# Windowed linear attention: masking part of the score lists by a product on VectorE in place of bias matmuls

## The chip, the cores and the metric

The kernel runs on one core of one Trainium2 chip. The metric is the time of one execution on the device in microseconds (us); lower is better. Engines are called PE (TensorE, its weight loads as PEld), DVE (VectorE), ACT (ScalarE), POOL (GpSimd) and SP (SyncE, here only a queue of DMAs).

## The reference

Two layers work on an image of 256 channels and 64 x 64 pixels in f32. Layer 0 is a windowed linear attention with a projection; layer 1 is a causal softmax attention over the 4096 pixels as tokens, with a feed-forward part, and then a mixture of experts. Only layer 0 is touched here. Cut to its core:

```python
q, k = sigmoid(Wq x), sigmoid(Wk x)             # 8 heads of 32 channels
v = Wv x;  v = v / max(norm(v), 1e-12)
Ik, Ikv = integral(k), integral(k v^T)          # sums over rows and columns
for w in (1, 2, 4):                             # window sides 64, 32, 16
    ws = 64 // w
    attn = q . box(Ikv, ws) / (q . box(Ik, ws) + 1e-6)
out = x + Wout concat(attn) + bout
```

For every query pixel this is the sum of (q.k) v over all key pixels inside a square window, divided by the sum of q.k.

## The kernel before, in words

The kernel doesn't form the box sums of k v^T at every pixel. It multiplies queries with the keys near the border of their window and then with the values, as an attention does, and takes what is entirely inside the windows from sums over blocks of 8 x 8 pixels. Only the border work is changed here.

**Head groups and stages.** `window_heads` runs twice, for heads 0 to 3 and 4 to 7. Each time it projects q, k and v, and then goes through two stages of border work. The *column stage* (windows of half 16 and 32, `beside`) treats key blocks at the left and right border. Its results go through DRAM (`store`, SP). The *row stage* (`above`, windows of half 8, 16, 32) treats the upper and lower border in eight strips of 8 image rows, Y = 0 to 7, and finishes each strip.

**Parts and lists.** A `Part` is one tile of 128 keys against a rectangle of 124 to 256 queries. `packed` puts two to three parts into a *list* of at most 512 queries, so that one head's scores of a list fill one PSUM bank. There are 44 lists in the column stage and 91 in the row stage of each head group, 135 in all, so 270 in the kernel. A part with `half` set has only half a tile of keys.

**`push(parts)`** handles one list. It takes four PSUM banks, one for each head. For each part and head it issues first a bf16 matmul (line 428) that writes a bias into the bank: 0 where the key lies in the query's window, at least -64 below it where not (`window_tables`). Then it issues the f32 score matmul (line 441), which adds q.k. Each f32 matmul stands in the trace as two records. Since q.k is positive and below 64, a ReLU of the sum leaves q.k inside the window and 0 outside. `evacuate` (lines 387 to 392) does that ReLU from PSUM into the buffer `pm`, one instruction for each head: five of eight on ACT, three of eight on DVE. `pm` shares a pool of three buffers (tag "work") with the raw image.

**`add()`** multiplies the oldest waiting `pm` with the values (line 474) into an accumulator bank. In `push`, `if len(waiting) > 1: add()` makes the products of a list follow the scores of the next one on PE. When an accumulator is complete, `finish` (row stage, DVE lines 506 and 509, POOL line 510) or `store` (column stage, ACT line 486) empties it.

**PSUM.** `Banks` hands out eight banks in turn. An accumulator holds one, so that about seven rotate. `push` takes four each time, and a bank can be written again when what was in it has been read.

**Order.** In these stages the order of PE, POOL, DVE and ACT is that of the program (`manual_schedule`); SP's order is set by the framework. In the row stage `plan(at, ...)` puts further work behind given lists: `outer` (DMAs of the column results), `inner` (block sums for a strip, DVE lines 574 to 582), `ahead` (box sums, POOL), `quarters` (DMAs of values), the steps of `norms` (PE, ACT, four DVE reciprocals of line 555), `convolve` (the projection of the strip before, PE line 589 and DVE line 594) and, in the second head group only, the layer norm of the strip before (`causal.measure`, `root`, `norm`, `turn`, `sum_up`). `spread_out` copies norms from PSUM (line 564).

**Memory that the change reuses.** The weights `l0Wq`, `l0Wk`, `l0Wv` are not read after the projections of a head group, nor is `going`, the start pattern of the running sums of line 614. A DMA for the next head group's image (`raw`) goes into a buffer of the pool "work".

## Time and profile before

| | us |
|---|---|
| time of three runs: median (lowest to highest) | 1775.1 (1774.4 to 1779.42) |
| the profiled execution: its time | 1775.84 |
| its span, first to last instruction | 1774.0 |
| column stage, first and second head group | about 82 to 178, 500 to 592 |
| row stage, first and second head group | about 178 to 437, 592 to 865 |
| layer 1 | from about 902 to the end |

The mean granted TensorE clock is 0.984 of full speed. Times in a profile are counted from the first instruction. A row of a group gives the line, engine and operation, out<-in, the count, the busy time (us) and the mean of one (ns), and behind the bar the idle time just before. Instructions of one engine can overlap by some ten ns, so that a group's busy time can be less than count times mean.

### The profile page before, as it was taken

The page shows a single profiled execution, that of the slowest core. Times are in us where ns is not written, and L with a number is a line of the kernel's source. Part 1 is how long each engine was busy: PE and PEld are TensorE (multiplying, and loading weights), DVE is VectorE, ACT ScalarE, POOL GpSimd, SP SyncE. Part 2 cuts the span into 40 slices and gives each one's busy share as a digit, 9 for nine tenths or more (in the row PEclk, how much of TensorE's full clock was granted, in tenths as well). Part 3 has the DMA queues.
Part 4 walks back from the last instruction along what each step waited for, and adds up shares of the span by engine and source line. Part 5 has one row for each costly group of instructions (what it writes and reads, how often), then busy time and mean ns, then how long its engine had stood idle before and what let it go on. Part 6 is the DMA issues. An engine that isn't in the chain of part 4 may idle for free.

```text
span 1774.0 us, 48097 instructions
## 1 busy us (share of the span) xinstructions
PE 1697.7 (96%) x20940; PEld 1252.7 (71%) x20940; DVE 989.3 (56%) x2002; ACT 789.5 (45%) x1478; POOL 518.7 (29%) x783
## 2 busy tenths in 40 slices
PE   4999999999999999999999999999999998699998
PEld 3666666666666666666777888788777777477877
DVE  5645666665744677777633446455655565634434
ACT  2566444444456644545223334444444445332232
POOL 2386434441274353333110312212112111122211
PEclk9999999999999999999999999999999998799999
DMA  7521211001331210002000000000000000100000
GB/s 241 138 74 50 57 28 38 20 21 48 125 91 44 73 28 24 24 22 73 3 0 1 1 0 1 1 1 0 1 0 1 1 1 1 48 12 24 13 24 24
DMA packets 82915, 61.13 MB, mean 34 GB/s; under 512 B 39120, under 2 KB 72808, under 8 KB 82704
## 3 DMA queue, kind: packets, MB, share of 16 engines
q1 hardware_dynamic: 77776, 47.61, 9.3%
q10 hardware_dynamic: 3664, 6.61, 1.1%
q0 software_dynamic: 1264, 3.84, 0.7%
q8 instruction: 164, 2.69, 0.6%
q14 instruction: 47, 0.39, 0.1%
HBM read 40.60 MB, written 17.44 MB: 33 GB/s over the span
## 4 chain that ended last, share of the span: by engine, by line
PE 87%; DVE 6%; ACT 3%; DMA 2%; issue 1%; POOL 0%; ACTq 0%; SPq 0%; DVEq 0%; POOLq 0%
PE ps L474 14%; PE ps L441 12%; PE pa L1162 11%; PE po L1235 10%; PE ph L1572 6%; PE py L1592 6%; PE ps L589 5%; PE ps L428 5%; PE ps L601 3%; PE ps L494 2%; PE pm L1296 2%; PE pm L1091 2%; PE ps L624 2%; PE pm L1305 1%; PE ps L560 1%
## 5 line engine op out<-in xcount | busy, mean ns | idle before, releaser
L390 ACT ACTIVATE pm<-ps 128x448 f32<-128x448 f32 (+22 forms) x674 | 323.7, 545 | 278.7 <-PE ps L441 163.0
L392 DVE TENSOR_SCALAR pm<-ps 128x448 f32<-128x448 f32 (+13 forms) x406 | 240.8, 621 | 202.9 <-PE ps L441 132.7
L441 PE MATMUL ps<-q,kh 32*128 32x188 f32 (+15 forms) x4224 | 205.7, 332 | 0.3 <-issue 0.3
L1162 PE MATMUL pa<-qT,k 128*128 128x256 f32 (+1 forms) x800 | 184.7, 375 | 0.0
L1178 DVE TENSOR_TENSOR max<-max,pa 128x512 f32<-128x512 f32 x105 | 71.8, 684 | 189.4 <-ACT s L1174 189.3
L1162 PEld LDWEIGHTS pa<-qT,k 128*128 128x128 f32 x800 | 150.2, 190 | 23.5 <-issue 2.2
L1214 ACT ACTIVATE s<-s 128x512 f32<-128x512 f32 x136 | 85.5, 630 | 179.2 <-DVE s L1213 175.5
L441 PEld LDWEIGHTS ps<-q,kh 32*128 32x128 f32 (+1 forms) x4224 | 145.4, 169 | 6.7 <-issue 4.2
L474 PE MATMUL ps<-pm,vh 128*32 128x188 f32 (+9 forms) x2688 | 148.4, 336 | 0.0
L510 POOL TENSOR_TENSOR y<-y,rn 128x512 f32<-128x512 f32 x32 | 41.1, 1283 | 329.1 <-DVE y L509 324.4
L1174 ACT COPY s<-pa 128x512 f32<-128x512 f32 x120 | 69.8, 582 | 114.9 <-PE pa L1162 114.8
L428 PE MATMUL ps<-table,table 32*128 32x256 bf16 (+19 forms) x2752 | 120.3, 252 | 0.0
L428 PEld LDWEIGHTS <-table 32*128 32x128 bf16 (+1 forms) x2752 | 48.0, 94 | 98.9 <-issue 96.0
L1592 PE MATMUL py<-w,hT 128*128 128x256 f32 x512 | 111.8, 379 | 0.0
L1592 PEld LDWEIGHTS py<-w,hT 128*128 128x128 f32 x512 | 97.3, 190 | 15.7 <-issue 1.9
L474 PEld LDWEIGHTS ps<-pm,vh 128*32 128x32 f32 x2688 | 71.1, 109 | 52.5 <-issue 34.7
L1235 PE MATMUL po<-kh,s 128*128 128x257 f32 x406 | 105.5, 388 | 2.4 <-ACT s L1214 2.4
L1213 DVE TENSOR_TENSOR s<-s,tops 128x512 f32<-128x512 f32 x136 | 95.2, 703 | 1.0 <-ACT tops L1206 1.0
L589 PE MATMUL ps<-l0wo,y 128*128 128x256 f32 x384 | 90.7, 387 | 0.0
L1235 PE MATMUL po<-v,s 128*128 128x257 f32 x342 | 87.6, 387 | 1.8 <-ACT s L1214 1.8
L1235 PEld LDWEIGHTS po<-kh,s 128*128 128x128 f32 x406 | 75.9, 194 | 15.9 <-ACT s L1214 3.8
L1597 DVE TENSOR_TENSOR y<-py,xn 128x256 f32<-128x256 f32 x32 | 13.6, 425 | 131.0 <-issue 78.1
(325 smaller groups left out, 3028.8 us busy)
## 6 DMA issues: line engine op xcount, KB each, us to landing
oscratch<-ov SPq DMA_DIRECT2D x32, 256.0 KB
ov<-oscratch SPq DMA_DIRECT2D x32, 256.0 KB
vq<-vscratch SPq DMA_DIRECT2D x80, 64.0 KB
t<-in_xT SPq DMA_DIRECT2D x16, 256.0 KB
vscratch<-v SPq DMA_DIRECT2D x32, 128.0 KB
vh<-vscratch SPq DMA_DIRECT2D x16, 256.0 KB
raw<-in_x ACTq DMA_DIRECT2D x7, 512.0 KB
raw<-in_x SPq DMA_DIRECT2D x7, 512.0 KB
```

The costliest lines, as they stand in the source:

```text
L390: nc.scalar.activation(dst, src, AF.Relu)
L392: nc.vector.tensor_scalar_max(dst, src, 0.0)
L428: nc.tensor.matmul(got[h][ps, spot].rearrange("p (y x) -> p y x", y=part.r1 - part.r0), lhsT=spread[hs, kind, ks], rhs=bias[hs], start=(i ...
L441: nc.tensor.matmul(got[h][ps, spot].rearrange("p (y x) -> p y x", y=part.r1 - part.r0), lhsT=keys[hs], rhs=q[hs, part.r0 : part.r1, part.c ...
L474: nc.tensor.matmul(out, lhsT=v, rhs=pm[:, h, spot].rearrange("p (y x) -> p y x", y=part.r1 - part.r0), start=fresh, stop=(left[key] == 0), ...
L589: nc.tensor.matmul(pt[:, i * D : (i + 1) * D], lhsT=ys[wi, Y][:, (2 * j + i) * P : (2 * j + i + 1) * P], rhs=wo[:, n, :], start=(n == 0), ...
L1162: nc.tensor.matmul(pp[:, k * 2 * P + at : (k + 1) * 2 * P], lhsT=key, rhs=qT[:, c, q0 + at : q0 + 2 * P], start=(c == 0), stop=(c == DC - 1))
L1213: nc.vector.tensor_tensor(s, s, u["top"].unsqueeze(1).to_broadcast([P, 2, 2 * P]), op=ALU.subtract)
L1214: nc.scalar.activation(u[b], u[b], AF.Exp, scale=1.0 / 16.0)
L1235: nc.tensor.matmul(acc, lhsT=u[b][:, (2 * k + j) * P : (2 * k + j + 1) * P], rhs=v[2 * b + k][:, 0 : D + 1], start=(b == h and k == 0), st ...
L1572: nc.tensor.matmul(ph, lhsT=w1v[:, e, c, f, :], rhs=x2[g][c], start=(c == 0), stop=(c == DC - 1))
L1592: nc.tensor.matmul(py, lhsT=hT[:, e, f, j * P : (j + 1) * P], rhs=w2v[:, e, f, :], start=(e + f == 0), stop=(e == 1 and f == FC - 1))
```

## The change

Of each head group's 135 lists, 60 are *masked*: 21 of the column stage (every second one from the third on) and 39 of the row stage (a list without half parts, never two in a row). For a masked list `push` issues no bias matmul; the first score matmul starts the bank. It is evacuated by DVE alone, with one `tensor_mul` for each part and head: scores in PSUM times a mask of bytes (1 inside, 0 outside) into `pm`. Each of the other 75 lists is evacuated by ACT alone, four ReLUs. The split of `evacuate` is gone.

The masks come from DRAM, five DMAs on SP's queue before the column stage's first list and one before the row stage, in each head group: into the memory of the weights (three), of `going` (two), and into a tile `near` of its own. The second head group fills `going` again (two memsets).

The products now follow two lists behind the scores (`len(waiting) > 2`), so all three buffers of "work" are in use. Between the stages the waiting products of the column stage are issued at once. In the row stage `outer` and `quarters` come one list later, and `convolve` with all that is chained to it too.

```diff
+MASKS = ("near", "beside 1", "beside 2", "beside 4", "above 1", "above 2")
+def inside_or_not():
+    spread, *tables = [o[0:32].astype(np.float32) for o in window_tables()]
+    kinds = [(0, tables[0]), (1, tables[3]), (1, tables[4]), (2, tables[5]), (0, tables[1]), (0, tables[2])]
+    masks = [np.tensordot(spread[:, kind], o, (0, 0)) == 0 for kind, o in kinds]
+    for n in (4, 5):
+        masks[n] = np.stack([masks[n][:, 0, 0:4, 16:-16], masks[n][:, 1, 4:8, 16:-16]], 1)
+    return masks
 def window_masks():
-    return window_tables()
+    return [*window_tables(), np.concatenate([m.reshape(P, -1) for m in inside_or_not()], 1).astype(np.uint8)]
...
+    shapes, masks = dict(zip(MASKS, inside_or_not())), {}
+    def load_mask(name, dst):
+        sizes = [int(np.prod(shapes[n].shape[1:])) for n in MASKS[: MASKS.index(name) + 1]]
+        dst = dst[:, 0 : sizes[-1]]
+        masks[name] = dst.rearrange("p (s y x) -> p s y x", s=shapes[name].shape[1], y=shapes[name].shape[2])
+        nc.sync.dma_start(out=dst, in_=a["mask7"][:, sum(sizes[:-1]) : sum(sizes)])
+        return sizes[-1]
+    def inside_of(part):
+        r, c = part.r0 + part.b0, part.c0 + part.d0
+        if part.vertical:
+            m = masks["beside 4" if part.half is not None else f"beside {part.wi}"]
+        elif part.wi == 0:
+            m = masks["near"]
+        else:
+            m, r, c = masks[f"above {part.wi}"], part.r0 % 4, c - 16
+        return m[:, part.side, r : r + part.r1 - part.r0, c : c + part.c1 - part.c0]
...
+    if hg:
+        nc.vector.memset(going, 1.0)
+        nc.vector.memset(going[:, :, 0:1], 0.0)
...
-    def push(parts):
+    def push(parts, masked=False):
...
-        for i, (part, spot) in enumerate(order):
+        for i, (part, spot) in enumerate([] if masked else order):
...
-                        start=False, stop=(i == len(parts) - 1), skip_group_check=True,
+                        start=(masked and i == 0), stop=(i == len(parts) - 1), skip_group_check=True,
...
         for h in range(4):
-            evacuate(pm[:, h, 0:at], got[h][:, 0:at])
+            if masked:
+                for part, spot in zip(parts, spots):
+                    rows = lambda s: s.rearrange("p (y x) -> p y x", y=part.r1 - part.r0)
+                    nc.vector.tensor_mul(rows(pm[:, h, spot]), rows(got[h][:, spot]), inside_of(part))
+            else:
+                nc.scalar.activation(pm[:, h, 0:at], got[h][:, 0:at], AF.Relu)
         waiting.append((parts, spots, pm))
-        if len(waiting) > 1:
+        if len(waiting) > 2:
             add()
...
+            for name, o in zip(("beside 1", "beside 2", "beside 4"), ws):
+                load_mask(name, o.rearrange("p c e -> p (c e)").bitcast(U8))
+            unused = going.rearrange("p y x -> p (y x)").bitcast(U8)
+            n = load_mask("above 1", unused)
+            load_mask("above 2", unused[:, n:])
             lists = packed(list(beside(wi, X)) for X in range(8) for wi in (1, 2))
...
-                push(parts)
+                push(parts, i % 2 == 1)
...
             push(lists[0])
+            while len(waiting) > 1:
+                add()
             by_rows(2)
             by_rows(3)
...
+        load_mask("near", h.tile([P, shapes["near"][0].size], U8, name="near"))
+        masked = [0]
+        for n in range(3, len(lists)):
+            if n > masked[-1] + 1 and all(part.half is None for part in lists[n]):
+                masked.append(n)
...
-            plan(at, lambda Y=Y: (outer(1, Y), outer(2, Y)))
+            plan(at + (1 if Y else 0), lambda Y=Y: (outer(1, Y), outer(2, Y)))
...
-                plan(at, lambda Y=Y: (ahead(Y + 1), quarters(Y + 1)))
+                plan(at, lambda Y=Y: ahead(Y + 1), lambda Y=Y: quarters(Y + 1))
...
-                end = plan(at + 3, *(lambda j=j, Y=Y: convolve(Y - 1, j) for j in range(2)))
+                end = plan(at + 4, *(lambda j=j, Y=Y: convolve(Y - 1, j) for j in range(2)))
...
-                push(parts)
+                push(parts, n in masked)
```

More of the change, by code (lines that the diff above doesn't have):

```diff
@@ L16 @@
 I32 = mybir.dt.int32
+U8 = mybir.dt.uint8
 AF = mybir.ActivationFunctionType
@@ L383, in window_heads @@
     ikv = big.tile([P, 9, 9, 32], F32, name="ikv")
-    counter = [0]
-    def evacuate(dst, src):
-        counter[0] += 1
-        if counter[0] % 8 in (1, 3, 5, 7, 0):
-            nc.scalar.activation(dst, src, AF.Relu)
-        else:
-            nc.vector.tensor_scalar_max(dst, src, 0.0)
     accs, left, state, ys, waiting = {}, {}, {}, {}, []
```

## The prediction

> **What bounds the kernel now.** I read the page first, then the busy time by stage, then the order in time of a few lists, and at last the groups that the change touches.

> ```profile
> PE 1697.7 (96%) x20940; PEld 1252.7 (71%) x20940; DVE 989.3 (56%) x2002; ACT 789.5 (45%) x1478; POOL 518.7 (29%) x783
> PE 87%; DVE 6%; ACT 3%; DMA 2%; issue 1%; POOL 0%; ACTq 0%; SPq 0%; DVEq 0%; POOLq 0%
> ```

> PE is busy 96% of the span, and the chain that ended last runs over it for 87%. That is a mean over stages. The four stages that the change touches (column and row stage of each head group) read so; behind the stretch stand its length and the busy time of PE, PEld, DVE, ACT and POOL:

> ```profile
> 82.00:178.00 96.00, 93.66 (x2094) 60.44 (x2096) 47.39 (x79) 63.44 (x133) 70.86 (x127) 0.98 0.19 61
> 178.00:437.00 259.00, 258.99 (x5847) 170.61 (x5846) 161.35 (x263) 120.89 (x247) 96.49 (x113) 1.00 0.13 31
> 500.00:592.00 92.00, 89.74 (x1982) 57.89 (x1986) 43.13 (x71) 59.15 (x123) 46.04 (x106) 0.96 0.19 60
> 592.00:865.00 273.00, 272.70 (x6028) 180.22 (x6023) 198.09 (x372) 132.76 (x274) 99.38 (x115) 1.00 0.15 37
> ```

> PE has no hole in either row stage. DVE is busy 62% and 73% there, 49% and 47% in the column stages. The order in time of a few lists on PE shows what a list consists of:

> ```profile
> 116.78 0.41 PE L428 MATMUL ps<-table,table 32*128 32x160 bf16 x12
> 117.03 1.04 PE L441 MATMUL ps<-q,k 32*128 32x168 f32 x24
> 118.00 0.96 PE L474 MATMUL ps<-pm,v 128*32 128x224 f32 x16
> 118.89 0.40 PE L428 MATMUL ps<-table,table 32*128 32x256 bf16 x8
> 119.12 0.98 PE L441 MATMUL ps<-q,k 32*128 32x224 f32 x16
> 120.03 1.05 PE L474 MATMUL ps<-pm,v 128*32 128x160 f32 x24
> 121.01 0.40 PE L428 MATMUL ps<-table,table 32*128 32x256 bf16 x8
> ```

> Bias, scores and products follow without a wait for the evacuation. What a bias costs is start to start: 119.12 - 118.89 = 0.23 us for two parts, 117.03 - 116.78 = 0.25 for three. Over all lists with nothing else between, these are 0.207 (8 matmuls) and 0.247 (12).

> **1. The removed bias matmuls.** Over both head groups 92 masked lists have two parts and 28 have three: 92 x 0.207 + 28 x 0.247 = 26.0 us of PE, all on the path. That is the upper end. The first weight load of a list is now that of a score, 185 ns (median of line 441) in place of 93 ns (line 428), and nothing may run under it: at worst 120 x 0.092 = 11.0 us come back, so the lower end is 15. I take half, **20.5 us gained**.

> **2. DVE's new work.** The nearest rows are DVE's present evacuation, and line 509, a tensor_tensor of PSUM with SBUF:

> ```profile
> 116.08 1.16 DVE L392 TENSOR_SCALAR pm<-ps 128x448 f32<-128x448 f32 x2 [1.43 <-PE ps L441]
> 300.28 0.68 DVE L509 TENSOR_TENSOR y<-ps,ov 128x512 f32<-128x512 f32 x1
> 300.87 0.94 DVE L555 RECIPROCAL r<-r 96x128 f32<-96x128 f32 x1
> ```

> One evacuation of 448 columns has a mean of 622 ns, yet two in a row take 1.16 us: the second starts 0.54 after the first. From the starts of such pairs the pitch is 441 ns at 352 columns, 541 at 448, 608 at 512: **73 ns + 1.045 ns a column**. The tensor_tensor behaves alike: 0.68 long, but the next starts 0.59 after it. Its 32 executions take 679 to 693 ns, so a busy POOL doesn't slow this form. A read of bytes isn't in the trace; I take f32's pace, since the same row holds for one tensor or two.

> A masked list of two parts of 224 then takes 4 x 2 x (0.073 + 0.234) = 2.46 us of DVE. The masked lists of a head group hold 46 + 88 parts and 9496 + 17504 columns: 184 x 0.073 + 37984 x 1.045 ns = 53.1 us in the column stage, 352 x 0.073 + 70016 x 1.045 ns = 98.9 in the row stage. The present evacuation leaves: 40.7 and 38.8 us of DVE in the column stages, 78.8 and 81.5 in the row stages. DVE becomes 59.8 of 96, 181.5 of 259, 57.4 of 92 and 215.5 of 273 us: 62%, 70%, 62%, 79%. So DVE doesn't become the bound on the mean.

> [...]

> **3. When banks come free.** Before, a list's four banks were emptied by two engines in some 1.2 us; now one engine takes 2.5 (DVE) or 4 x 0.44 = 1.8 (ACT, from its pitch of 441 ns at 448 columns). With seven banks rotating, the scores of list n+2 need three of list n's banks and one of n+1's. Two lists of 448 columns take PE 2 x 2.0 - 0.2 = 3.8 us by the rows above, scores last about 0.9, so the need comes 2.9 us after the end of list n's scores; DVE is done at about 2.5 + 0.1. That is 0.3 to 0.4 of slack for each masked list. The second list of lag covers the products: list n's come after the scores of n+2. So strict alternation costs nothing by itself. What is queued on DVE behind a masked list does: `inner` (3.1 us for both windows in the first strip), four reciprocals (0.94 each), `finish` (0.6 each), `convolve`'s add (0.6 each), and in the second head group the layer norm, (198.1 - 81.5) - (161.4 - 78.8) = 34 us, some 5 a strip.

> I walked through strip Y = 2 (lists 20 to 32, six masked). Lists 20-21: DVE 3.9, PE 4.9 us. 22-23, with `inner`: DVE 5.4 to 6.8, PE 3.9. 24-25: DVE 3.4, PE 9.0, as `convolve` (2.8 x 2) now lies there and hides most of the backlog; about 0.4 is lost. 26-27 and 28-29: DVE 4.5, PE 5.0. 30-32: DVE 5.8, PE 5.6. So 0.3 to 0.4 us is lost in a strip of the first group: 2 us in all. In the second, 26-27 and 28-29 become 5.9 on DVE against 5.0 and 5.1, which loses another 0.5 and 0.8 in the three strips with six masked lists: 5 us in all. The column stages have only `norms`' reciprocals near their end and the turns of accumulators: 1 us.

> **4. Queues.** Five mask DMAs stand on SP before the first list. A DMA issue of this queue takes some 0.6 us, and the nearest small one, 64 KB into `kh`, lands 2.88 us after its issue at 90.65. The first masked list's product is due at about 92, so DVE, and behind it PE, can wait up to 3 us in each head group if the masks lie behind `kh`, and nothing if the framework puts them ahead: 0 to 6 us, I take 2. `raw` for the second head group waits for a buffer of "work" one list longer; PE idles for it today (about 439.6 to 442.3): 0 to 2 us, I take 1. `outer`, `quarters` and `near` are covered: `finish` for `ov` comes eight lists, some 16 us, later; without that cover one landing of about 3 us would show. Filling `going` again is under 1 us of DVE before the scans, while PE waits for `raw` anyway. The changed place of `convolve` costs nothing of its own. ACT evacuates with 300 instructions a head group in place of 337, so it is no bound.

> **The sum.** -20.5 + 2 + 5 + 1 + 2 + 1 = -9.5 us. From the profiled 1775.84 that is 1766.3; the median of the runs lies 0.7 below the profiled one, so **1766 us**.

> **Rivals.**
> - *Everything is hidden.* The backlog vanishes in places where PE does other work, the masks are early, the weight load overlaps: 26 - 2 = 24 us gained, **1751**. For it: DVE at 70 to 79% and slack in every pair. Against it: the bursts of strip Y = 2.
> - *Bank release becomes the wait (slower).* DVE is in order, and one `inner` or two reciprocals in front of a masked list hold four banks. If each of the 14 strips with such bursts loses 2.3 us (one `inner` of 1.5 to 2.4 us and some rest) in place of 0.5, that is 32 us: 1775 - 20.5 + 32 + 3 = **1790**. It decides from 1.3 us a strip on. The same comes about if the products run at their full duration (143 ns + 1.06 a column, from the same rows) and not at the pitch: a masked list then takes 3.2 us, over the 2.9 that PE leaves. For it: DVE's 79% is a mean, and in three strips of the second group it is near 90% (strip Y = 2, 661 to 699 us: DVE 29.2 busy, 11.2 of it evacuation, 15.2 in its place, so 33.2 of 38 - 1.2).
> - *No net change.* The lower end of the saving, 15 us, meets 10 to 15 us of waits, late masks among them: **1774**.

> **How the numbers follow.** The forecast has 0.38, all hidden 0.15, bank release 0.32, no net change 0.15. A measurement tells about 0.3% (5.3 us) from no change. The forecast's own range is 1758 to 1773. Faster by more: 0.30 of the forecast and all of the second case, 0.45. Within 0.3%: the forecast's remainder and the last case, 0.23. Slower: 0.32. The range reaches to the case with all hidden below, and to the slower case with 2 us on top: 1751 to 1792.

> **What the profile would show.** Line 428 falls from 2752 to 1680 records. The product comes as a DVE group of 1072 instructions with 224 columns at about 0.31 us of pitch. If step 1 is right, the start of a masked list's score follows the products with no more than 0.1 us beyond today's 0.25. If step 3 is right, PE stays over 97% busy in the row stages, and the second is the worse one. If the slower rival is right, PE shows waits before line 441 that end with DVE's product, most of them behind lines 574 to 582 and 555. A masked list that waits for a DMA in the first 15 us of a column stage would show step 4. Wrong would be: a pitch over 0.36 us for 224 columns, or a second column stage that grows.

## The result, and the profile after

| | before | after |
|---|---|---|
| median of four runs each (us) | 1775.97 (1774.4 to 1779.42) | 1835.79 (1831.82 to 1837.91) |
| ratio, with its 95% interval | | 1.0331 (1.0307 to 1.0356) |
| profiled execution: time, span (us) | 1775.84, 1774.0 | 1831.82, 1830.0 |
| mean granted TensorE clock | 0.984 | 0.975 |

The change made the kernel slower by 3.3%, some 60 us. The forecast was 1766, and its range ended at 1792.

Line numbers from here on are those of the changed kernel: bias 456, score 469, masked product 479, ACT's ReLU 481, products with the values 507, `finish` 542 (DVE) and 543 (POOL), box sums 556 to 571, copy of the norms 597, `convolve` 622 and 627.

The head of the page of the changed kernel:

```profile
span 1830.0 us, 46546 instructions
PE 1717.3 (94%) x19868; PEld 1264.9 (69%) x19868; DVE 1050.5 (57%) x2670; ACT 744.8 (41%) x1404; POOL 518.1 (28%) x783
```

PE has 1072 records fewer and is nevertheless busy 19.6 us longer: the matmuls themselves became slower. The stages, in the columns that the prediction used (stretch, length, busy time of PE, PEld, DVE, ACT and POOL, granted clock, DMA share, GB/s):

```profile
82.00:175.00 93.00, 89.20 (x1838) 57.36 (x1838) 58.80 (x191) 52.57 (x109) 67.92 (x120) 1.00 0.20 66
175.00:464.00 289.00, 272.65 (x5534) 180.35 (x5530) 184.45 (x481) 108.44 (x231) 98.22 (x118) 0.96 0.11 28
529.00:623.00 94.00, 89.57 (x1839) 57.66 (x1832) 59.88 (x194) 53.00 (x111) 48.19 (x111) 1.00 0.20 63
623.00:917.00 294.00, 279.21 (x5559) 184.34 (x5559) 205.61 (x572) 116.69 (x248) 97.69 (x114) 0.97 0.14 34
```

The column stages changed by less than 2 us. The row stages grew from some 261 and 269 us to 289 and 293. PE was without a hole in them before (0.3 us in both); now it stands idle for 16 and 15 us, and the granted clock fell to 0.96 and 0.97 on the mean. DVE, the engine that received the new work, is busy 64% and 70% there: it is not the bound.

Three rows of the waits (who waited <- for whom; the engine's idle time before it in us in total, times, longest) name the place. The last two are the same waits, seen on PE's weight loads and on its matmuls:

```profile
ACT rn L597 <- POOL y L543: 67.9, 12, 8.2
PEld ps L469 <- ACT rn L597: 29.2, 10, 4.4
PE ps L469 <- ACT rn L597: 26.5, 10, 4.1
```

None of them existed before. There ACT's copy of the norms waited for PE's norms, and a few times for less than 0.8 us for something else; and POOL's multiply of `finish` stood ahead of the box sums (a row of the waits, and two rows in time of the same strip, from the kernel before):

```profile
ACT rn L564 <- PE ps L560: 21.9, 26, 1.2
```

```profile
234.90 1.29 POOL L510 TENSOR_TENSOR y<-y,rn 128x512 f32<-128x512 f32 x1 [6.71 <-DVE y L509]
236.14 1.29 POOL L525 TENSOR_TENSOR rows<-ik 128x520 f32<-128x520 f32 x1
```

Now ACT's copy waits for POOL's multiply, and the scores wait for ACT's copy. The order in time of one such place in the changed kernel, the strip whose `convolve` starts at 244.22 (rows between are left out):

```profile
233.38 0.68 DVE L542 TENSOR_TENSOR y<-ps,ov 128x512 f32<-128x512 f32 x1
...
238.95 1.34 POOL L571 TENSOR_TENSOR box<-box,q 128x512 f32<-128x512 f32 x1
...
240.26 1.25 POOL L543 TENSOR_TENSOR y<-y,rn 128x512 f32<-128x512 f32 x1
...
241.55 0.59 ACT L597 COPY rn<-ps 128x512 f32<-128x512 f32 x1 [6.26 <-POOL y L543]
...
242.19 1.25 PE L469 MATMUL ps<-q,kh 32*128 32x168 f32 x12 [2.26 <-ACT rn L597]
...
244.22 4.47 PE L622 MATMUL ps<-l0wo,y 128*128 128x256 f32 x12
```

DVE has finished its half of `finish` at 234.06. POOL's multiply needs 1.25 us and could run at once, but in POOL's program order the box sums of `ahead` stand in front of it until 240.3. The next strip's norms are copied into the very buffer `rn` that this multiply reads, so ACT's copy waits for it. ACT is idle for 6.26 us before the copy; the norms lay ready at 237.69, so that 3.9 us of these are POOL's (over all 12 copies, 43.6 of the 67.9 us). The copy also empties the PSUM bank in which PE wrote the norms. Banks are handed out in turn, and this one falls to the third of the four heads of the list that PE has begun: the scores of two heads are done, and PE stands from 239.93 to 242.19, when the copy has just ended. The ReLUs that empty the other banks stand behind the copy in ACT's order. Then follows something that costs more than half as much again. The same place by windows, in the columns of the stage table:

```profile
240.00:242.00 2.00, 0.00 (x0) 0.00 (x0) 1.93 (x3) 0.45 (x1) 1.51 (x2) 1.00 0.00 0
242.00:244.00 2.00, 1.81 (x28) 1.29 (x28) 1.10 (x6) 1.65 (x5) 0.00 (x0) 1.00 0.00 0
244.00:248.00 4.00, 4.00 (x18) 3.11 (x11) 1.26 (x6) 0.00 (x0) 0.00 (x0) 0.57 0.02 4
248.00:252.00 4.00, 4.00 (x63) 2.96 (x62) 0.69 (x1) 1.95 (x4) 0.00 (x0) 1.00 0.00 0
```

PE is idle for two microseconds at full clock, works again, and *then* gets a clock of 0.57 on the mean of four microseconds (0.5 for 3.413 us of them). The twelve matmuls of `convolve` that fall there last 4.47 us; the next twelve, at 250.59, last 2.86.

The loss in the row stages is the sum of both. Idle: 31.1 us from the records (the expectations below have 31.6), against 0.3 before. Half clock: four intervals of 3.413 us and four of 6.827, 41 us in all, and none before; at a granted clock of 0.5 that loses an estimated 20.5. Together 52 us, where the row stages, counted from list to list, grew by 27.2 and 24.6 us.

### The profile page after: what moved, and what is told of

Its sections match the earlier page's. It is cut to its first block, busy times and chain, and to the rows that moved or that the text cites. A ratio compares the mean times of both kernels' runs of the same rounds, so it can differ in the third digit from the quotient of the medians.

```text
span 1830.0 us, 46546 instructions
## 1 busy us (share of the span) xinstructions
PE 1717.3 (94%) x19868; PEld 1264.9 (69%) x19868; DVE 1050.5 (57%) x2670; ACT 744.8 (41%) x1404; POOL 518.1 (28%) x783
## 4 chain that ended last, share of the span: by engine, by line
PE 46%; DVE 7%; issue 2%; ACT 2%; POOL 1%; ACTq 0%; DVEq 0%; POOLq 0%
PE pa L1207 11%; PE po L1280 10%; PE ph L1617 6%; PE py L1637 6%; PE ps L469 2%; PE pm L1341 2%; PE pm L1136 2%; PE ps L507 1%; PE pm L1350 1%; PE ps L622 1%; DVE lnst L900 1%; DVE max L1223 1%; PE pm L1064 1%; DVE pm L479 1%; ACT s L1219 1%
## 5 line engine op out<-in xcount | busy, mean ns | idle before, releaser
L481 ACT ACTIVATE pm<-ps 128x448 f32<-128x448 f32 (+12 forms) x600 | 278.0, 551 | 285.1 <-issue 187.4
L469 PE MATMUL ps<-q,kh 32*128 32x188 f32 (+15 forms) x4224 | 231.0, 340 | 28.9 <-ACT rn L597 26.5
L469 PEld LDWEIGHTS ps<-q,kh 32*128 32x128 f32 (+1 forms) x4224 | 163.4, 170 | 62.5 <-ACT rn L597 29.2
L507 PE MATMUL ps<-pm,vh 128*32 128x188 f32 (+9 forms) x2688 | 154.3, 344 | 0.6 <-ACT pm L481 0.5
L479 DVE TENSOR_TENSOR pm<-ps,going 128x188 f32<-128x188 f32 (+5 forms) x368 | 100.3, 347 | 35.6 <-PE ps L469 32.6
L479 DVE TENSOR_TENSOR pm<-ps,near 128x184 f32<-128x184 f32 (+4 forms) x336 | 99.2, 367 | 36.4 <-ACT pm L481 20.2
L622 PE MATMUL ps<-l0wo,y 128*128 128x256 f32 x384 | 99.0, 412 | 0.0
L622 PEld LDWEIGHTS ps<-l0wo,y 128*128 128x128 f32 x384 | 76.6, 206 | 21.1 <-issue 10.4
L1642 DVE TENSOR_TENSOR y<-py,xn 128x256 f32<-128x256 f32 x32 | 13.6, 425 | 130.7 <-issue 78.1
```

Of the source, the lines that this page charges most:

```text
L469: nc.tensor.matmul(got[h][ps, spot].rearrange("p (y x) -> p y x", y=part.r1 - part.r0), lhsT=keys[hs], rhs=q[hs, part.r0 : part.r1, part.c ...
L479: nc.vector.tensor_mul(rows(pm[:, h, spot]), rows(got[h][:, spot]), inside_of(part))
L481: nc.scalar.activation(pm[:, h, 0:at], got[h][:, 0:at], AF.Relu)
L507: nc.tensor.matmul(out, lhsT=v, rhs=pm[:, h, spot].rearrange("p (y x) -> p y x", y=part.r1 - part.r0), start=fresh, stop=(left[key] == 0), ...
L622: nc.tensor.matmul(pt[:, i * D : (i + 1) * D], lhsT=ys[wi, Y][:, (2 * j + i) * P : (2 * j + i + 1) * P], rhs=wo[:, n, :], start=(n == 0), ...
```

## The experiments

**Theories.** A: `ahead(Y + 1)` is still planned at list `at`, but `finish` of the strip before now comes one list later, as products follow two lists behind. So on POOL the box sums went from behind that multiply to in front of it, and everything above follows. B: DVE's masked products (or ACT's four ReLUs in a row) release banks late, and the copy's wait is only a by-product. C: the lag of two itself costs.

**The mended order.** Only the place of the box sums changes; the DMAs of `quarters` stay one list behind `at`, where the change had put them.

```diff
-                plan(at, lambda Y=Y: ahead(Y + 1), lambda Y=Y: quarters(Y + 1))
+                plan(at + 1, lambda Y=Y: (ahead(Y + 1), quarters(Y + 1)))
```

> The changed kernel with one edit: the box sums for the next strip (ahead, about 11.5 us of POOL work) are put one list later, so that on POOL's queue they stand behind the multiplication by rn of the last result of the strip before, as they did before the change. Theory A (POOL's order: the multiplication waits behind the box sums, ACT's copy of the next rn waits for it, ACT's queued evacuations hold the banks, PE idles and its granted clock falls to 0.5 afterwards): the copy's waits for POOL, 67.9 us in 12 times, go below 10 us, PE's idle time in the row stages goes from 31.6 us to below 6, and the time falls from 1836 us to 1765 to 1785. Theory B (bank release: one engine empties all four banks and DVE's other work lies in front): POOL's order is a side effect, the strips stay about 6 us longer than before, and the time stays above 1805 us.

Measured: 1781.57 us, 1.0037 (1.0024 to 1.005) times before. The same place in its order in time:

```profile
234.38 0.68 DVE L542 TENSOR_TENSOR y<-ps,ov 128x512 f32<-128x512 f32 x1
235.21 1.27 POOL L543 TENSOR_TENSOR y<-y,rn 128x512 f32<-128x512 f32 x1 [5.34 <-ACT pm L481]
...
236.44 1.30 POOL L558 TENSOR_TENSOR rows<-ik 128x520 f32<-128x520 f32 x1
...
238.78 0.59 ACT L597 COPY rn<-ps 128x512 f32<-128x512 f32 x1 [2.49 <-PE ps L593]
...
242.02 2.86 PE L622 MATMUL ps<-l0wo,y 128*128 128x256 f32 x12
```

The multiply now starts right behind DVE's add and the box sums follow it; the twelve matmuls are back at 2.86 us, and no half clock is left in the row stages. In the whole kernel ACT's copy now waits for PE alone:

```profile
ACT rn L597 <- PE ps L593: 34.8, 18, 2.5
```

Its stages, in the columns of the table above:

```profile
82.00:175.00 93.00, 89.12 (x1839) 57.06 (x1835) 59.67 (x194) 52.95 (x112) 68.04 (x121) 1.00 0.21 67
175.00:437.00 262.00, 261.40 (x5602) 173.71 (x5600) 184.39 (x483) 109.84 (x235) 101.25 (x120) 1.00 0.13 32
500.00:594.00 94.00, 89.74 (x1843) 57.51 (x1839) 59.71 (x194) 53.08 (x112) 48.15 (x112) 1.00 0.19 64
594.00:872.00 278.00, 273.46 (x5650) 180.34 (x5642) 211.22 (x582) 118.37 (x252) 100.15 (x115) 1.00 0.14 36
```

One list's difference in the place of one task is worth 54 us of the 60. DVE has the same masked products as in the changed kernel, 184.4 against 184.5 us in the first row stage, and there PE is busy 261.4 of 262. B falls as the main cause.

**The order without the masks.** All lists keep their biases and the old split evacuation; the lag of two and the shifted plan stay.

```diff
-                push(parts, n in masked)
+                push(parts)
...
-                nc.scalar.activation(pm[:, h, 0:at], got[h][:, 0:at], AF.Relu)
+                evacuate(pm[:, h, 0:at], got[h][:, 0:at])
```

> The lag of two lists and the shifted plan without any mask product: all lists have their bias matmuls, and the evacuation is split over ACT and DVE as before the change (the mask DMAs remain). Theory A (POOL's order): most of the loss is there without a single masked list; 1805 to 1840 us. Theory B (bank release by a single engine): the banks are emptied by two engines as before, so the time is that of before within 0.5%, 1767 to 1785 us.

Measured: 1829.57 us, 1.0303 (1.0282 to 1.0323). Without a single masked list nearly the whole loss is there. A row of its waits, and the shares of the chain of waits:

```profile
ACT rn L606 <- POOL y L552: 50.8, 12, 6.8
```

```profile
PE 68%; issue 13%; POOL 8%; DVE 6%; ACT 3%; DMA 2%; ACTq 0%; POOLq 0%; DVEq 0%; SPq 0%
```

The copy (line 606 here) waits for the multiply (552) 12 times, as in the changed kernel, and POOL holds 8% of the chain, where before it held 0% (and holds 0% again in the next run).

**The same with the mended order.** The kernel just shown, with the edit of the first experiment.

> Lag of two and the shifted plan without masked lists (split evacuation, all biases), but with the box sums one list later. It completes the square of masks or not, POOL's order wrong or mended. Theory A (POOL's order is the loss, masks are a small matter by themselves): 1774 to 1784 us, against 1829.6 with the wrong order; what is left over the time before is the later image load for the second head group, 1 to 5 us. Theory B (the lag of two costs by itself, by banks or buffers): 1795 us or more.

Measured: 1779.13 us, 1.0023 (1.0012 to 1.0033). With it the square is complete:

| times before | biases | masks |
|---|---|---|
| box sums in front of `finish` | 1.0303 | 1.0331 |
| box sums behind it | 1.0023 | 1.0037 |

The order costs 2.8 to 2.9% with or without masks. The masks cost 0.1 to 0.3% net, and in the lower row the two intervals overlap. The lag of two, with the shifted plan and the DMAs of the masks, costs 0.2% even in the mended order and without masks.

**The reverse: the kernel before, with only the box sums put earlier.**

```diff
-                plan(at, lambda Y=Y: (ahead(Y + 1), quarters(Y + 1)))
+                plan(max(at - 1, 0), lambda Y=Y: ahead(Y + 1))
+                plan(at, lambda Y=Y: quarters(Y + 1))
```

> The kernel before with one edit: the box sums for the next strip are put one list earlier, so that POOL's order is that of the changed kernel, while lag, bias matmuls and evacuation are as before. Theory A: the copy of rn on ACT now waits for POOL in most strips, but the copy comes three lists behind the box sums and not two, so the waits are 3 to 6 us and not 6 to 8; 1790 to 1820 us. Theory B: nothing of what it needs is changed; 1770 to 1782 us.

Measured: 1783.15 us, 1.0034 (1.0021 to 1.0047). The row of the waits appears:

```profile
ACT rn L564 <- POOL y L510: 23.5, 9, 4.6
```

The direction is right and the size was missed (1790 to 1820 was expected). In this kernel the copy stands one list further behind `finish`, its longest wait is 4.6 us in place of 8.2, and no score waits for it. PE's largest holes in the row stages, 2.38 and 1.54 us, come by another link: `convolve` (line 589), which reads `y`, waits for the late multiply itself.

```profile
318.16 4.39 PE L589 MATMUL ps<-l0wo,y 128*128 128x256 f32 x12 [2.38 <-POOL y L510]
```

Each hole is followed by 3.4 us of half clock. So the wrong order alone doesn't fix the price; how late POOL's multiply is for the next one that needs it does.

**The multiply taken off POOL.** The changed kernel, with `finish` wholly on DVE.

```diff
-            nc.gpsimd.tensor_mul(o, o, rn)
+            nc.vector.tensor_mul(o, o, rn)
```

> The changed kernel, its plan untouched, with one edit: the multiplication by rn in finish is done by DVE and not by POOL, so that nothing of a finished strip stands behind the box sums. It breaks the same chain at another link. Theory A: ACT's copy of rn no longer waits for POOL, PE's idle time falls from 31.6 to below 10 us, and the time goes to 1780 to 1795 us, a little above the mended order for 1.4 us more of DVE in each strip. If the box sums hurt in another way (POOL and DVE slowing each other, say), the time stays above 1815.

Measured: 1794.45 us, 1.0114 (1.0096 to 1.0132).

```profile
ACT rn L597 <- PE ps L593: 38.9, 18, 3.9
```

The box sums are still where the change put them, but nothing that the copy needs stands behind them: it waits for PE alone, and 41 us come back (1835.79 - 1794.45). What remains against the mended order, 13 us (9 in the profiled spans), is seen in part as idle PE in the row stages, 3.6 and 8.2 us against 0.6 and 4.0, somewhat above the 10 that were expected, and as one half-clock interval of 3.4 us in each. The longest hole of each stage, 1.7 us, waits for the last reciprocal of the norms, which now stands behind the multiply on DVE:

```profile
205.12 1.13 PE L593 MATMUL ps<-r,spreadh 32*128 32x512 f32 x4 [1.68 <-DVE r L588]
```

The rest was not followed up.

**The masks in the old order.** Masked lists, but products one list behind and the plan of before.

```diff
-        if len(waiting) > 2:
+        if len(waiting) > 1:
...
-                end = plan(at + 4, *(lambda j=j, Y=Y: convolve(Y - 1, j) for j in range(2)))
+                end = plan(at + 3, *(lambda j=j, Y=Y: convolve(Y - 1, j) for j in range(2)))
```

> The masked lists alone: 60 of 135 lists without bias matmuls and multiplied by bytes on DVE, but products one list behind the scores and the plan as before the change, so that POOL's order is the old one. Theory A: no POOL wait; the products of a masked list now come right after the next list's scores, when DVE has emptied only part of it, so PE waits up to 1.3 us at each of 120 lists, partly covered: 1770 to 1830 us, without waits of the rn copy for POOL. Theory B: as in the changed kernel or worse, above 1825 us.

Measured: 1798.54 us, 1.012 (1.0098 to 1.0142).

```profile
PEld ps L507 <- DVE pm L479: 11.9, 41, 0.5
```

Here ACT's copies don't wait for POOL's multiply (DVE's copies do 7 times, 1.5 us at the longest), but 41 weight loads of products wait for the masked product of the list just scored, 11.9 us in all; in the mended order 4 do, 0.9 us. That is a part of the difference; the rest was not located. So C falls as the cause: with masks the lag of two is worth 17 us (1798.54 - 1781.57), once the box sums go along with it.

**What the saving is.** The kernel before, with the biases of the masked lists left out and no masking in their place (keys outside the window then count in these lists).

```diff
-        for i, (part, spot) in enumerate(order):
+        for i, (part, spot) in enumerate([] if masked else order):
```

> The kernel before, where the 60 lists of each head group that the change masks have no bias matmuls, and everything else (split ReLU evacuation, lag of one, plan) is as before. What is left out: the masking of those lists. It measures the gain of the removed matmuls by itself. The prediction's step 1 took 20.5 us of 26.0; then 1755. In the trace with the box sums put one list later, a masked list's time from its first matmul to the products is shorter than before by a median of 0.104 us in the column stage and 0.118 in the row stage; then 42 x 0.104 + 78 x 0.118 = 13.6 us are gained: 1760 to 1764.

Measured: 1758.9 us, 0.9915 (0.99 to 0.9929), so 15.1 us (12.6 to 17.8) of 1776.06. This is all that the change could gain if everything that it adds were hidden.

**Where the mended order loses it again.** First, masks only up to the end of the first row stage; the second has biases and split evacuation. Then, in addition, the last four lists of the first row stage leave only one list waiting, so that the buffers of "work" are free sooner for the next image. Then, in addition, the second row stage with a lag of one and the old plan (`lag[0] = 2 - hg`, and every place of the plan less `hg`).

```diff
-                push(parts, n in masked)
+                push(parts, n in masked and hg == 0)
+                if hg == 0 and n >= len(lists) - 4:
+                    while len(waiting) > 1:
+                        add()
```

> Box sums one list later, masked lists in both column stages and in the first head group's row stage only; the second row stage has all its biases and the split evacuation. If the 7.2 us that this stage is longer than before (278.2 against 271.0 us) come from DVE, which has the layer norm there as well, the stage goes back to 271 to 273 us and the whole to 1772 to 1776. If they come from the lag or the plan, it stays at 276 to 279, and the whole at 1779 to 1783.

> As the kernel with masked lists in both column stages and the first row stage and with the box sums one list later; in addition the last four lists of the first row stage are multiplied one list behind, so that the buffers for the second head group's image come free as before. With the mended order the stretch from the last list of the first row stage to the first of the second column stage is 66.3 us against 60.2 before. If the late buffers are the cause, it goes back to 60 to 62, and the whole to 1774 to 1777 us; if the order of DVE's work there is, it stays, and so does the time, 1778 to 1782.

> The best that the runs point to: masks, lag of two and the mended order where they gained (both column stages, 0.5 and 2 us; first row stage, 3 us), the early tail, and in the second row stage all as before the change. If these gains add up, 1768 to 1773 us, 0.2 to 0.4% under the kernel before; if the stretch between the head groups keeps its 6 us, 1774 to 1779.

| | us | times before | row stage 1 | between the groups | row stage 2 |
|---|---|---|---|---|---|
| before | | | 261.4 | 60.7 | 268.8 |
| mended order, no masks | 1779.13 | 1.0023 (1.0012 to 1.0033) | 261.3 | 65.4 | 268.2 |
| mended order | 1781.57 | 1.0037 (1.0024 to 1.005) | 258.1 | 66.7 | 272.6 |
| masks not in row stage 2 | 1780.24 | 1.0027 (1.0014 to 1.0041) | 258.6 | 66.2 | 270.7 |
| with the early tail too | 1778.4 | 1.0007 (0.9995 to 1.0019) | 260.7 | 61.3 | 270.5 |
| lag of one in row stage 2 too | 1775.44 | 0.9996 (0.9983 to 1.0009) | 260.8 | 61.3 | 270.6 |

The stages are counted in the profiled execution from first to last score. The early tail does what was expected of it between the groups: the 6 us were buffers of "work" held one list longer, and they come back, though 2 us of them are paid in the row stage before. Only a part of the 6 us is the wait itself: PE's hole there is 4.6 us in the mended order and 2.7 before, and behind the longer one stand 6.8 us of half clock, an estimated 3.4 us lost; with the early tail the hole is 2.4 us, without half clock.

In the second row stage the lag and the plan cost nothing without masks (268.2 us), so the 272.6 come with the masks. But some 2 us stay when only that stage has none, with either lag, and why stays open. The hoped-for whole was missed in all three, in the second by 1.4 us: no version that masks is faster than the kernel before.

## Why the prediction was wrong

**Step 4 failed, in what it left out.** It asks what each moved step is put past, and answers for SP's DMAs, for `raw`, and for `convolve` ("costs nothing of its own"). The step that was moved past another queue is none of these. `finish` is called by `add`, and `add` moved one list later while `ahead` kept its list: POOL's order of the two turned round, which the diff doesn't show in a line. The prediction had `ov`'s `finish` in its hand ("comes eight lists, some 16 us, later") and asked only for its DMA. Step 3 walked strip Y = 2 list by list, but only on DVE and PE. Had POOL been walked too, from the trace of before, the danger was there to see: some 11.5 us of box sums would come in front of a multiply that stood ahead of them, and behind it stood a copy that waited for little but PE. Nor did the prediction price an idle PE at more than its own length; the half clock added an estimated 20.5 us to 31.1 of idle. Neither of the two signs that it named as "Wrong would be" showed: the pitch was 0.30 us, and the second column stage didn't grow. They watched DVE, and the loss came by POOL.

**The slower rival** ended on the right side and had the right last link, banks that are released late. It put the cause into DVE, at 2.3 us a strip and 1790. Neither holds: the scores wait for DVE's product for 5.9 us in the whole changed kernel, 18 times, 0.4 at the longest, and what holds the bank is ACT's copy, behind POOL. The range, made of that rival and 2 us, ended 44 us short.

**Step 1: right kind, too large.** 20.5 us was taken from 15 to 26; the saving alone measured 15.1. From the starts of the lists, a masked list gains a median 0.104 us in the column stages and 0.118 in the row stages: 42 x 0.104 + 78 x 0.118 = 13.6 us, which lies within the 12.6 to 17.8. What comes back, 0.207 - 0.104 = 0.103 us a list, is about the 0.092 of a weight load that is wholly exposed (185 ns in place of 93): the lower end was the value. The scores of one list of a column stage of the changed kernel, and the products behind them:

```profile
104.30 1.04 PE L469 MATMUL ps<-q,k 32*128 32x224 f32 x16
105.27 0.96 PE L507 MATMUL ps<-pm,v 128*32 128x224 f32 x16
```

From the first score to the products it is 0.97 us; the same list in the kernel before needs 1.09 from its first bias.

**Step 2: right.** The prediction gave 0.307 us for a product of 224 columns, and 59.8, 181.5, 57.4 and 215.5 us of DVE in the four stages. The rows show 58.8, 184.5, 59.9 and 205.6 (the last is 211.2 in the mended order, whose stretch takes in more of what follows), and one masked list so:

```profile
100.90 2.48 DVE L479 TENSOR_TENSOR pm<-ps,l0Wk 128x224 f32<-128x224 f32 x8 [1.77 <-PE ps L469]
```

Eight products in 2.48 us, the last of them 0.38: a pitch of (2.48 - 0.38) / 7 = 0.30. At 224 columns, bytes as second operand cost nothing beyond the f32 pitch of 0.307.

**Step 3: right in kind, too small.** In the mended order, where it can be seen alone, the stages lose against the saving of 13.6 us: 1.7 and 0.3 us in the columns (predicted 1 in all), 1.3 in the first row stage (2), 8.5 in the second (5). Of these 8.5, 1.9 remain when that stage has no masks. As holes of PE only 4.0 us of them are seen, which end mostly with ACT's ReLUs, DVE's masked products and its layer norm; the rest is not located. The 0.3 of the second column stage is flattered: the kernel before has 6.8 us of half clock there, an estimated 3.4 us, and the mended order has its own before that stage, between the groups.

**Step 4's other terms.** Late masks: 2 us were taken, none seen; the first masked list's product waits for its scores. The buffer of "work" between the groups: 1 us was taken, 6.0 measured, of which an estimated 3.4 are half clock. Line 456 has 1680 records, as predicted.

**The sum again,** from the parts in the mended order: -13.6 + 1.7 + 0.3 + 1.3 + 8.5 + 6.0 = +4.2 us, where the spans differ by 6.0. So without the failed step the forecast would still have been some 14 to 16 us too low (4.2 + 9.5 by the stages, 1781.6 against 1766 by the medians), from three mis-sized terms: the saving, the second row stage and the buffers.

## What to carry to other kernels

Where a program's order is every engine's order, delaying one step by a list moves everything that this step calls, on every engine; list for each engine what the step was ahead of and is now behind, the lightly loaded ones too (POOL is busy 28% here, and its order alone cost 54 us). Follow the write-after-read of single buffers through such a queue until it reaches the engine that bounds. And price an idle gap of TensorE with the half clock that may follow it, not by its length alone: in the row stages here 31.1 us of idle PE came with 41 us of half clock, an estimated 20.5 us more.

## What the hardware showed that was not expected

In the first row stage of the changed kernel, idle gaps of PE of 2.26, 3.00 and 2.23 us were each followed by 3.413 us of half clock, and gaps of 4.12 and 4.14 us each by 6.827 us. The half clock began 2.4 to 4.2 us after the start of the gap, in three of the five when PE was busy again: the gap of 239.93 to 242.19 has its half clock from 244.1 to 247.5. The matmuls that look slow there, the twelve of `convolve` with 4.47 us in place of 2.86, are not those that waited.
